# Decoder layer in f32 on one core: the first batch element's cross-attention output projection as seven block products, and its transposed weights copied by two engines

## The chip, the cores and the metric

The kernel runs on one core of one Trainium2 chip. The metric is the device time of one execution in microseconds (us). TensorE (PE in the profile, its weight loads PEld) does the matrix products, VectorE (DVE), ScalarE (ACT) and GpSimd (POOL) the elementwise work, and SyncE (SP) issues nearly all DMAs.

## The reference, cut to what matters

A decoder layer for a batch of 2, 512 tokens, width 512, all in f32: self-attention of 16 heads with block-scaled weights, then cross-attention on a context of 1024 rows in which each token keeps its 54 highest scores, then a gated feed-forward part. After each comes a residual sum and a layer norm. The piece that matters here is the end of the cross-attention:

```python
scores = coef * jnp.einsum('bsd,bnd->bsn', Q, K_mem)
thr = jax.lax.top_k(scores, clip_k)[0][..., -1:]
att = jax.nn.softmax(jnp.where(scores < thr, -jnp.inf, scores), axis=-1)
out = jnp.einsum('bsn,bnd->bsd', att, V_mem)      # 512 x 1024 by 1024 x 512
return out @ W_o.T                                # 512 x 512 by 512 x 512
x = _layernorm(x + that)
```

## The kernel before, in words

Most matrix products are done as **seven block products**: both operands are cut into 2 by 2 blocks, seven products of sums and differences of blocks take the place of the eight plain ones, and the results are put together by additions. `combine_a` and `combine_b` (lines 104 to 120) make the four sums of the left or of the right operand; `sums_a` (line 137) does it in steps, and overwrites one block. `seven` (line 170) issues the products for one block of 128 output rows by two column halves of 256:

- products 1, 6 and 7 build up in one PSUM bank `r`. After each of them ScalarE copies the bank's running state out into `u` (`keep`, line 197), and the next of the three has to wait for that copy.
- products 2 and 4, then 5 and 3, go to three quarters of a double bank `z`. When 2, 4 and 5 are there, `on_second` adds `z` and `u` on VectorE. Product 3 builds up on product 5 in the same place, so it waits until `on_second` has read it. It is left open (`rest`, line 222), and the next `seven`, or `close()`, issues it. Then `on_first` adds.
- with `late=True`, products 2 and 4 are issued ahead of product 1.

The program's order is not the order on the engines. A planner orders each engine's instructions when the kernel is built: in the trace POOL runs the sums of line 1214 at 689.7 us and those of line 1211 at 702.4 us, and matrix products of different calls alternate on PE. The order of the program acts as a priority.

The cross-attention of the **second** element (b = 1, at 863 to 903 us) uses seven block products throughout, the output projection too: `xattend` line 607 on. `xw["woc"]` (line 1222) are the sums of the output weights, made on GpSimd in place `v1`. The **first** element (b = 0, at 652 to 711 us) goes like this:

- `transpose_weights` (line 541): the 512 by 1024 softmax weights are transposed on PE, 32 transposes of 128 by 128 into PSUM (line 552); each group of four fills a bank, and ScalarE copies the bank to SBUF (line 555). There are 8 such copies. `combine_at` then makes the sums of the transposed weights on VectorE (lines 152 to 155).
- `xattend(0)` (line 578) is a generator. Its first step, `xav0_0`, is run at line 1036. Then come `project(last)`, the end of the self-attention of element 1; its layer norm; `turn_x(1)` (line 1039), which transposes element 1's activations with VectorE transposes and 16 small DMAs into `x1T`; `combine_turned` (line 1040, the sums `x1c`) and loads.
- at line 1043 the second half of `xattend(0)` follows: `xav0_1`, and then the output projection, which for b = 0 is **plain**: 4 token tiles by 4 chunks, 16 products of 128 by 128 by 512 (line 633) into banks `r` and `t`, in an order that uses the chunks `ot` 0, 2 and 3 before the last one, `ot` 1. VectorE adds each tile to the residual (line 642).
- then `layernorm(0)`, the transposition `x2T` and the sums `x2c` for element 0's feed-forward part, and on PE meanwhile `seven_xquery(1)` (products named xq, from `x1T`, `x1c` and the GpSimd sums `wqc`) and `seven_xscores(1)` (named xs).

Places in SBUF are shared by name: `wv` holds the sums `oc` of `project(last)` until its last product, `k0`, `q0`, `q1` hold keys and queries of attention heads, and later `ut` and `gt` of the feed-forward part.

Of the kernel before, what the change touches and what calls it, by code (L numbers as in the profile page):

```python
# [16 lines left out]
P = 128  # L17
# [7 lines left out]
def decoder_layer(  # L25
# [21 lines left out]
    nc = tc.nc  # L47
# [4 lines left out]
    NT = S // P  # L52
    NK = M // P
# [6 lines left out]
    HK, HS, HD = KD // 2, S // 2, D // 2  # L60
# [11 lines left out]
    def bank(tag, name):  # L72
        return ps.tile([P, 512], F32, tag=tag, name=name)
# [4 lines left out]
    def place(tag, shape, name):  # L78
        return sb.tile([P, *shape], F32, tag=tag, name=name)
# [21 lines left out]
    ALEFT = lambda a, c: {1: a[0], 2: a[1], 3: c[3], 4: a[3], 5: c[0], 6: c[1], 7: c[2]}  # L101
# [11 lines left out]
    def combine_b(eng, b, c):  # L113
        b00, b01, b10, b11 = b
        c = [c[:, n] for n in range(4)]
        eng.tensor_tensor(c[0], b01, b00, ALU.subtract)  # L116
        eng.tensor_tensor(c[1], b11, c[0], ALU.subtract)
        eng.tensor_tensor(c[2], b11, b01, ALU.subtract)
        eng.tensor_tensor(c[3], b10, c[1], ALU.subtract)
        return BRIGHT(b, c)  # L120

    def blocks(w):

        k, n = w.shape[1] // 2, w.shape[2] // 2
        return w[:, :k, :n], w[:, :k, n:], w[:, k:, :n], w[:, k:, n:]
# [11 lines left out]
    def sums_a(eng, a, c, steps):  # L137


        for n, w in enumerate(steps):  # L140
            a00, a01, a10, a11 = (f[:, w] for f in a)
            eng.tensor_tensor(c[0][n], a10, a11, ALU.add)
            eng.tensor_tensor(c[1][n], c[0][n], a00, ALU.subtract)
            yield
            eng.tensor_tensor(a10, a00, a10, ALU.subtract)
            eng.tensor_tensor(c[2][n], a01, c[1][n], ALU.subtract)
            yield
# [17 lines left out]
    def close():  # L165

        if open_product:
            open_product.pop()()

    def seven(name, stat, mov, cols, on_second, on_first, bias=(0.0, 0.0), late=False, piece=None, scale=1.0):  # L170


        n = seven_count[0] % 2
        seven_count[0] += 1
        r = bank("r", f"r{name}")[:, :HS]
        if piece:

            zs = [bank("t", f"z{name}_{i}")[:, :HS] for i in range(2)] + [double(f"z{name}", (4, HS))[:, 2, :]]
        else:
            z = double(f"z{name}", (4, HS))  # L180
            zs = [z[:, i, :] for i in range(3)]
        u = place(f"u{n}", (3, HS), f"u{name}")

        def product(i, o, start=True):
            left, right = chunks(stat[i]), chunks(mov[i])
            for k in range(len(left)):
                nc.tensor.matmul(  # L187
                    o,
                    left[k][:, cols],
                    right[k],  # L190
                    start=start and k == 0,
                    stop=k == len(left) - 1,
                    skip_group_check=not start,
                )

        def keep(i, at, scale=1.0):
            nc.scalar.activation(u[:, i, :], r, AF.Identity, bias=at, scale=scale)  # L197

        if late:
            product(2, zs[1])  # L200
            product(4, zs[0])
        product(1, r)
        keep(0, bias[0])
        if not late:
            product(2, zs[1])
        product(5, zs[2])
        product(6, r, False)
        keep(1, bias[0])
        close()
        product(7, r, False)  # L210
        keep(2, bias[1], scale)
        if piece:
            piece(zs[2], u[:, 2, :], 1, 1)
            piece(zs[1], u[:, 0, :], 0, 0)
        if not late:
            product(4, zs[0])
        if piece:
            piece(zs[0], u[:, 2, :], 1, 0)
        else:
            on_second(z[:, 0::2, :], u[:, 2:3, :].to_broadcast([P, 2, HS]))  # L220

        def rest():
            product(3, zs[2], False)
            if piece:
                piece(zs[2], u[:, 1, :], 0, 1)
            else:
                on_first(z[:, 1:3, :], u[:, 0:2, :])

        open_product.append(rest)

    res, rb, xts, xcs = {}, {}, {}, {}
# [118 lines left out]
    mems, memTs, xw, qts, sts, ats = {}, {}, {}, {}, {}, {}  # L350
# [10 lines left out]
    def load_mem(b):  # L361
        mems[b] = []
        for n in range(2):
            mt = place(f"{('mt', 'pt')[b]}{n}", (NK // 2, D), f"mem{b}_{n}")
            nc.sync.dma_start(
                out=mt,
                in_=mem[b, n * half_m : (n + 1) * half_m, :].rearrange("(k p) f -> p k f", p=P),
            )
            mems[b].append(mt)
# [171 lines left out]
    def transpose_weights(b, tags):  # L541

        at = []
        for k in range(NK):
            if k % (NK // 2) == 0:
                ath = place(tags[k // (NK // 2)], (NK // 2, S), f"at{b}_{k}")
                at.append(ath)
            if k % 2 == 0:
                trs = double(f"atr{b}_{k}")
            tr = trs[:, k % 2, :]  # L550
            for t in range(NT):
                nc.tensor.transpose(
                    tr[:, t * P : (t + 1) * P], sts[b, t][:, k * P : (k + 1) * P], ident
                )
            nc.scalar.copy(ath[:, k % (NK // 2), :], tr)
        ats[b] = [a[:, :, h] for a in at for h in (slice(0, HS), slice(HS, S))]

    def combine_mem(b, tags):
# [15 lines left out]
    def combine_at(b, tags):  # L574
        c = [place(tag, (NK // 2, HS), f"atc{b}_{n}") for n, tag in enumerate(tags)]
        ats[b] = sums_b(nc.vector, ats[b], c)

    def xattend(b, ot_tags):

        oth = [place(tag, (2, S), f"xo{b}_{n}") for n, tag in enumerate(ot_tags)]  # L580
        ot = [t[:, n, :] for t in oth for n in range(2)]
        o4, sums = [t[:, :, h] for h in (slice(0, HS), slice(HS, S)) for t in oth], []
        if b == 1:
            c12 = [place(f"p{n}", (HK, HS), f"xoc{n}") for n in range(2)]
            c4 = place("wqk0", (HK, HS), "xoc_4")

        def first(z, u, m):
            put(ot[m], z, u, b == 1)
            if b == 1:
                c = [f[:, m : m + 1] for f in (*c12, c4)]  # L590
                sums.append(sums_a(nc.vector, o4, [[f] for f in c], [slice(m, m + 1)]))
                next(sums[-1])
                for left in sums if m else ():
                    next(left)

        for m in range(HK):
            seven(
                f"xav{b}_{m}",
                mems[b],
                ats[b],  # L600
                slice(m * P, (m + 1) * P),
                lambda z, u, m=m: put(ot[HK + m], z, u, b == 1),
                lambda z, u, m=m: first(z, u, m),
            )
            yield
        close()
        if b == 1:
            stat = ALEFT(o4, (*c12, o4[2], c4))
            for s in range(NT // 2):

                def add(z, u, t):
                    o = res[b, t].rearrange("p (c f) -> p c f", c=2)
                    nc.vector.tensor_add(o, o, u)
                    nc.vector.tensor_add(o, z, o)

                seven(
                    f"xpo{b}_{s}",
                    stat,
                    xw["woc"],
                    slice(s * P, (s + 1) * P),  # L620
                    lambda z, u, s=s: add(z, u, 2 + s),
                    lambda z, u, s=s: add(z, u, s),
                    late=s == 0,
                )
            close()
            return

        order = [(t, k) for t in range(NT) for k in (0, 2, 3, 1)]
        if b == 0:
            order = [(0, 0), (0, 2), (0, 3), (1, 0), (1, 2), (1, 3), (0, 1), (1, 1)] + order[8:]  # L630
        po = [bank("rt"[t % 2], f"xpo{b}_{t}") for t in range(NT)]
        for t, k in order:
            nc.tensor.matmul(
                po[t],
                ot[k][:, t * P : (t + 1) * P],
                xw["wo"][:, k, :],
                start=(k == 0),
                stop=(k == 1),
                skip_group_check=True,
            )  # L640
            if k == 1:
                nc.vector.tensor_add(res[b, t], po[t], res[b, t])

# [394 lines left out]
    combine_turned(nc.vector, 1, "v0", "x1")  # L1040
    load_xw("wq", xwq, "cmb1", 1)
    load_mem(1)
    for _ in attended:
        pass
    combine_memT(1, ("wqk3", "wqk4", "ot1"))
# [173 lines left out]
    load_wdn(0, 1)  # L1219
    search1 = chain(search1, turn_weights(1, 2, ("ot0", "ot1"), ("cmb0", "cmb1"), ("v0", "work")))  # L1220
    def attended_early():
        xw["woc"] = combine_b(nc.gpsimd, blocks(xw["wo"]), place("v1", (4, HK, HD), "woc"))
        yield from xattend(1, ("ot0", "ot1"))

    hc = up(0, 1, nc.vector, search1, combine_wdn(0, 1), attended_early())
# [86 lines left out]
```

## Time and profile before

| what | value |
|---|---|
| median of 3 runs | 1084.7 us (1083.64 to 1084.9) |
| profiled execution: its own time | 1084.43 us |
| its span, first to last instruction | 1082.6 us (1.83 us lie around it) |
| mean granted clock of TensorE | 0.999 |
| DVE, ACT, POOL busy | 57%, 38%, 53% of the span |
| stretch of the transposes on PE | 652.04 to 659.36 us |
| from the first to the last product of line 633 | 692.95 to 710.13 us |

A line of a timeline holds the start, the duration, the engine, the line, the operation, the tiles (output, arrow, inputs) and how many instructions were merged; brackets hold the idle time just before and what ended it. Every f32 matrix product shows as two records on PE, so the 16 products of line 633 are 32 records and the 32 transposes happen to be 32. The duration of a PE record overlaps the next one; the distance from start to start is its price.

### The profile page before, as it was taken

How to read it: one execution, taken by the hardware profiler on the slowest of the kernel's cores; microseconds unless marked ns; L12 is line 12 of the kernel's file. 1: busy time of each engine (PE TensorE's matmuls, PEld its weight loads, DVE VectorE, ACT ScalarE, POOL GpSimd, SP SyncE). 2: the span in 40 equal slices, each digit the busy share in tenths (PEclk: the TensorE clock that was granted, in tenths of full speed). 3: DMA queues.
4: the chain of work that ended last, by engine and by line, in shares of the span. 5: the costliest groups of instructions: out<-in, count | busy, mean ns of one | idle time of the engine just before them, and what ended most of it. 6: DMA issues, size and time to landing. Idle time of an engine off the chain costs nothing.

```text
span 1082.6 us, 12783 instructions
## 1 busy us (share of the span) xinstructions
PE 1070.4 (99%) x4252; PEld 796.8 (74%) x4252; DVE 613.4 (57%) x1015; ACT 409.0 (38%) x882; POOL 575.2 (53%) x578
## 2 busy tenths in 40 slices
PE   9999999999999999999999999999999999999997
PEld 5676776677677677665666567778888888888886
DVE  6444345335434445643899774468999736554354
ACT  3444435335344533733444453222443214221121
POOL 4966626846845856514952654525565812264530
PEclk9999999999999999999999999999999999999999
DMA  9545455655554455536332447231214401422201
GB/s 350 156 127 173 157 155 181 192 158 152 191 177 115 155 178 151 192 80 180 137 117 78 117 133 257 82 113 39 96 65 132 136 21 49 165 80 79 95 20 39
DMA packets 66097, 142.71 MB, mean 132 GB/s; under 512 B 12528, under 2 KB 12528, under 8 KB 66032
## 3 DMA queue, kind: packets, MB, share of 16 engines
q1 hardware_dynamic: 65312, 139.80, 41.6%
q10 hardware_dynamic: 720, 2.10, 0.5%
q8 instruction: 34, 0.56, 0.2%
q14 instruction: 31, 0.25, 0.1%
HBM read 99.90 MB, written 2.10 MB: 94 GB/s over the span
## 4 chain that ended last, share of the span: by engine, by line
PE 84%; DVE 10%; ACT 2%; DMA 1%; POOL 1%; issue 1%; SPq 0%; ACTq 0%; DVEq 0%; POOLq 0%
PE sc L785 10%; PE av L830 9%; PE zqk L187 9%; PE zgu L187 7%; PE rqk L187 7%; PE rgu L187 5%; PE zo L187 5%; PE zv L187 5%; PE zpd L187 4%; PE ro L187 4%; PE rpd L187 3%; PE rv L187 3%; DVE work L493 3%; PE zxav L187 3%; DVE top L496 2%; PE xs L474 2%
## 5 line engine op out<-in xcount | busy, mean ns | idle before, releaser
L830 PE MATMUL av<-pt,v 128*128 128x512 f32 x256 | 121.9, 592 | 0.0
L796 DVE TENSOR_REDUCE nm<-sc 128x2 f32<-128x1024 f32 x63 | 77.0, 1223 | 76.0 <-PE sc L785 75.8
L785 PE MATMUL sc<-k,q 128*128 128x512 f32 x256 | 116.9, 598 | 0.0
L799 ACT ACTIVATE p<-sc,nm 128x512 f32<-128x512 f32 x128 | 86.9, 681 | 76.7 <-DVE nm L796 76.6
L810 DVE STREAM_TRANSPOSE tq<-p 128x512 f32<-128x512 f32 x128 | 84.9, 700 | 37.9 <-ACT p L807 33.0
L785 PEld LDWEIGHTS sc<-k,q 128*128 128x128 f32 x256 | 47.3, 190 | 62.6 <-issue 51.3
L807 ACT ACTIVATE p<-p,sm 128x512 f32<-128x512 f32 x128 | 85.4, 715 | 1.6 <-DVE sm L806 1.4
L107 POOL TENSOR_TENSOR wc<-wgu 128x256 f32<-128x256 f32 x32 | 25.0, 781 | 112.8 <-PE zgu L187 69.1
L684 POOL TENSOR_TENSOR wqk<-wqk,sqk 128x512 f32<-128x512 f32 x52 | 66.1, 1290 | 33.6 <-DMA wqk<-in_wqk 20.7
L197 ACT ACTIVATE ugu<-rgu 128x256 f32<-128x256 f32 x96 | 36.2, 379 | 102.7 <-PE rgu L187 100.4
L830 PEld LDWEIGHTS av<-pt,v 128*128 128x128 f32 x256 | 48.6, 190 | 29.7 <-issue 25.8
L187 PE MATMUL rgu<-x2c,wc 128*128 128x256 f32 x256 | 66.1, 380 | 1.0 <-ACT ugu L197 1.0
L187 PE MATMUL rqk<-x0c,wc 128*128 128x256 f32 x248 | 65.0, 384 | 0.3 <-ACT uqk L197 0.2
L496 DVE MAX8 top<-work 128x8 f32<-128x1024 f32 x48 | 58.6, 1221 | 0.9
L848 ACT ACTIVATE ot<-av,bqkv_sb 128x512 f32<-128x512 f32 x28 | 19.2, 687 | 101.9 <-PE av L830 101.9
L187 PEld LDWEIGHTS rgu<-x2c,wc 128*128 128x128 f32 x256 | 48.3, 190 | 8.7 <-ACT ugu L197 1.5
L187 PEld LDWEIGHTS rqk<-x0c,wc 128*128 128x128 f32 x248 | 45.1, 189 | 12.2 <-ACT uqk L197 5.1
L107 POOL TENSOR_TENSOR wc<-wqk 128x256 f32<-128x256 f32 x31 | 22.7, 733 | 59.0 <-PE zqk L187 58.2
L116 POOL TENSOR_TENSOR otc<-ot 128x512 f32<-128x512 f32 x7 | 8.9, 1272 | 81.4 <-PE zv L187 81.4
L1136 DVE TENSOR_TENSOR gt<-zgu,ugu 128x512 f32<-128x512 f32 x32 | 21.9, 684 | 47.6 <-PE zgu L187 47.6
L493 DVE MATCH_REPLACE8 work<-top,work 128x1024 f32<-128x1024 f32 x40 | 48.3, 1209 | 0.0
L748 DVE TENSOR_TENSOR q<-zqk,uqk 128x512 f32<-128x512 f32 x31 | 21.3, 688 | 41.5 <-PE zqk L187 41.5
(313 smaller groups left out, 2477.9 us busy)
## 6 DMA issues: line engine op xcount, KB each, us to landing
pt<-tq SPq DMA_DIRECT2D x512, 64.0 KB, 2.0
wgu<-in_wgu SPq DMA_DIRECT2D x32, 512.0 KB, 3.3
wqk<-in_wqk SPq DMA_DIRECT2D x26, 512.0 KB, 5.9
sqk<-in_wqk_s SPq DMA_DIRECT2D x26, 512.0 KB, 4.2
wdn<-in_wdn SPq DMA_DIRECT2D x8, 1024.0 KB, 5.8
sv<-in_wv_s SPq DMA_DIRECT2D x14, 512.0 KB, 6.2
wv<-in_wv SPq DMA_DIRECT2D x7, 1024.0 KB, 5.2
wo<-in_wo SPq DMA_DIRECT2D x7, 1024.0 KB, 5.8
```

The source lines that it names most:

```text
L107: eng.tensor_tensor(c[0], a10, a11, ALU.add)
L187: nc.tensor.matmul(o, left[k][:, cols], right[k], start=start and k == 0, stop=k == len(left) - 1, skip_group_check=not start,)
L197: nc.scalar.activation(u[:, i, :], r, AF.Identity, bias=at, scale=scale)
L493: nc.vector.match_replace(work, top, src, LOWEST)
L496: nc.vector.max(top, work)
L684: eng.tensor_tensor(part[:, w], codes[:, w], sct[:, w], ALU.mult)
L785: nc.tensor.matmul(pair[n], q[:, (t + n) * P : (t + n + 1) * P], k, start=True, stop=True,)
L796: nc.vector.reduce_max(nms, scs, axis=AX.X, negate=True)
L799: nc.scalar.activation(pr, pair[t % 2], AF.Exp, bias=nms[:, t % 2 : t % 2 + 1], accum_out=sm,)
L807: nc.scalar.activation(pr, pr, AF.Copy, scale=sm)
L810: nc.vector.transpose(tq[:, :, :, t, :].rearrange("p n k c -> p k n c"), pr.rearrange("p (k n a) -> p k n a", n=NB, a=BLK),)
L830: nc.tensor.matmul(av, vs[u // GH][:, k, j * P : (j + 1) * P], pt[:, :, k, :], start=(k == 0), stop=(k == NT - 1),)
```

## The change

For b = 0 the output projection takes the path that b = 1 had. The attention output's sums go to places `q0`, `q1`, `k0`; the sums of the output weights are made once more for b = 0, in place `wv`, on GpSimd, ahead of the second half of `xattend(0)`. The plain projection is gone. Of the 8 copies of the transposed weights, ScalarE does those with even k, VectorE those with odd k.

```diff
-            nc.scalar.copy(ath[:, k % (NK // 2), :], tr)
+            copy = nc.vector.tensor_copy if k % 2 else nc.scalar.copy
+            copy(ath[:, k % (NK // 2), :], tr)
...
+    def combine_wo(b, tag):
+        xw["woc"] = combine_b(nc.gpsimd, blocks(xw["wo"]), place(tag, (4, HK, HD), f"woc{b}"))
...
-        if b == 1:
-            c12 = [place(f"p{n}", (HK, HS), f"xoc{n}") for n in range(2)]
-            c4 = place("wqk0", (HK, HS), "xoc_4")
+        c12 = [place(f"{'qp'[b]}{n}", (HK, HS), f"xoc{b}_{n}") for n in range(2)]
+        c4 = place(("k0", "wqk0")[b], (HK, HS), f"xoc{b}_4")
...
             put(ot[m], z, u, b == 1)
-            if b == 1:
-                c = [f[:, m : m + 1] for f in (*c12, c4)]
-                sums.append(sums_a(nc.vector, o4, [[f] for f in c], [slice(m, m + 1)]))
-                next(sums[-1])
-                for left in sums if m else ():
-                    next(left)
+            c = [f[:, m : m + 1] for f in (*c12, c4)]
+            sums.append(sums_a(nc.vector, o4, [[f] for f in c], [slice(m, m + 1)]))
+            next(sums[-1])
+            for left in sums if m else ():
+                next(left)
...
-        order = [(t, k) for t in range(NT) for k in (0, 2, 3, 1)]
-        if b == 0:
-            order = [(0, 0), (0, 2), (0, 3), (1, 0), (1, 2), (1, 3), (0, 1), (1, 1)] + order[8:]
-        po = [bank("rt"[t % 2], f"xpo{b}_{t}") for t in range(NT)]
-        for t, k in order:
-            nc.tensor.matmul(
...
-            if k == 1:
-                nc.vector.tensor_add(res[b, t], po[t], res[b, t])
...
     load_mem(1)
+    combine_wo(0, "wv")
     for _ in attended:
         pass
...
-        xw["woc"] = combine_b(nc.gpsimd, blocks(xw["wo"]), place("v1", (4, HK, HD), "woc"))
+        combine_wo(1, "v1")
```

The loop `for s in range(NT // 2)` with `seven(f"xpo{b}_{s}", ...)` of lines 608 to 625 stays as it was, and now runs for both elements.

More of the change, by code (lines that the diff above doesn't have):

```diff
@@ L606, in xattend, with add @@
         close()
[L607 to L626, printed above, removed]
-        order = [(t, k) for t in range(NT) for k in (0, 2, 3, 1)]
-        if b == 0:
-            order = [(0, 0), (0, 2), (0, 3), (1, 0), (1, 2), (1, 3), (0, 1), (1, 1)] + order[8:]
-        po = [bank("rt"[t % 2], f"xpo{b}_{t}") for t in range(NT)]
-        for t, k in order:
[L633 to L639, printed above, removed]
-            )
-            if k == 1:
-                nc.vector.tensor_add(res[b, t], po[t], res[b, t])
+        stat = ALEFT(o4, (*c12, o4[2], c4))
+        for s in range(NT // 2):
+            def add(z, u, t):
+                o = res[b, t].rearrange("p (c f) -> p c f", c=2)
+                nc.vector.tensor_add(o, o, u)
+                nc.vector.tensor_add(o, z, o)
+            seven(
+                f"xpo{b}_{s}",
+                stat,
+                xw["woc"],
+                slice(s * P, (s + 1) * P),
+                lambda z, u, s=s: add(z, u, 2 + s),
+                lambda z, u, s=s: add(z, u, s),
+                late=s == 0,
+            )
+        close()
     phases = [(0, 0), (0, 1)] + [(g, b) for b in range(B) for g in range(1, NG)]
```

## The prediction

> **What bounds the kernel now.** I read the busy times first, then PE's own waits.
>
> ```profile
> PE 1070.4 (99%) x4252; PEld 796.8 (74%) x4252; DVE 613.4 (57%) x1015; ACT 409.0 (38%) x882; POOL 575.2 (53%) x578
> ```
> ```profile
> PE idle L86 <- DVE eps L90: 1.2, 1, 1.2
> PE rgu L187 <- ACT ugu L197: 1.0, 2, 0.7
> ...
> PE atr L552 <- ACT at L555: 0.4, 1, 0.4
> ```
>
> PE is busy 99% of the span, and each of its waits for another engine sums to 1.2 us or less. So a microsecond of products taken off PE is a microsecond of time if PE finds its next operands ready, and a bubble if it doesn't. The change touches two places; I read PE's timeline at the first and the chain that ended last at the second.
>
> ```profile
> 652.04 1.04 PE L552 MATMUL atr<-ident,s 128*128 128x128 f32 x8
> 653.46 0.66 PE L552 MATMUL atr<-ident,s 128*128 128x128 f32 x4 [0.38 <-ACT at L555]
> ...
> 659.36 3.60 PE L830 MATMUL av<-pt,v 128*128 128x512 f32 x8
> ```
> ```profile
> 693.11 0.86 PE xpo L633 x2
> ...
> 695.69 1.72 PE xpo L633 x4
> 697.41 1.73 PE zxav L187 x8
> 699.14 11.16 PE xpo L633 x26
> 710.29 0.86 PE rxq L187 x4
> ```
>
> In the first, PE waits for ScalarE to empty a bank. In the second PE runs without a hole, and six records of the projection sit between products of xav0_1, where they cover waits.
>
> **Part 1, the copies.** From 652.04 to 659.36 us, 7.32 us, PE does 32 transposes and 14 records of 256 columns. Transposes cost 0.108 each (four from 658.06 to 658.49), records of 256 columns 0.2157 (eight in the chain's 1.73): 3.45 + 3.02 = 6.47. So **0.85 us** is lost to the copies. ScalarE's eight take 0.586 each, behind an `ot_last` eviction of 0.69. Afterwards each engine has four. VectorE idles there (5.35 and 2.37 us before its sums `atc`), so they are hidden. No row shows a VectorE copy out of PSUM; the nearest, the 512-wide add that reads PSUM (L393, 0.69), and ScalarE's 0.586 bound it. The next thing, `av`, needs DMAs whose last issue ends at 654.5, plus 2.0 to landing: 656.5, before PE gets there at 658.5. Between nothing and -0.85 I take **-0.7**, since the bank pair is still filled and emptied alternately.
>
> **Part 2, the products.** Removed are 32 records of 512 columns at 11.16/26 = 0.4292: 13.73 us. Added are 2 x 7 x 2 = 28 products, 56 records at 0.2157: 12.08. **-1.65 us** of PE work.
>
> **Part 3, waits inside the new chain.** The plain order needed nothing back from ScalarE or VectorE; the seven need it at three places.
> (a) Between products 7 and 3 of xav0_1 PE waits for a copy and an add, from 695.53 to about 696.9, 1.37 us. Six plain records covered it and the step before. Now product 2 and product 1 of both halves can give only their first chunk there (the second needs `ot` 3 or `ot` 1): 3 x 0.43 = 1.29 in all. Bounds 0 to 0.6, taken 0.3.
> (b) After xav0_1's last product (698.97) `ot` 1 is put by 699.86; product 2's second chunk and product 4 cover 1.29. Taken 0.
> (c) The last product 3 waits for the add `on_second`. The second element shows it:
>
> ```profile
> 899.06 1.03 PE L187 MATMUL zxpo<-woc,xo 128*128 128x256 f32 x4
> 899.92 1.03 PE L187 MATMUL rgu<-x2T,wgu 128*128 128x256 f32 x4
> 900.78 0.59 PE L187 MATMUL zgu<-x2T,wgu 128*128 128x256 f32 x2
> 901.30 1.13 PE L187 MATMUL zxpo<-wo,xoc 128*128 128x256 f32 x4
> ```
>
> From 899.92 to 901.30, 1.38 us, the feed-forward part fills in. For the first element the only filler is xq, and that needs `x1T`:
>
> ```profile
> 693.60 13.06 SPq L289 DMA_DIRECT2D x1T<-x1Tt  x16
> ```
>
> The last issue ends at 706.66, plus a median 2.0 to landing: 708.7, or 708.0 shifted by part 1. PE would be at the hole at 710.13 - 1.65 - 0.7 - 0.86 = 706.9. So xq comes too late to cover it: bounds 0 (`x1T` lands earlier) to 1.4, taken **1.0**, since xq can fill the hole's end. (a) and (c): **+1.3**.
>
> **Part 4, the other engines.** VectorE adds 8 sums of 0.42 (L142 to L146), and 8 adds of 0.69 take the place of 4: +6.1 us. From 699.2 to 726.4 it is busy 17.9 of 27.2, so the other 9.3 hide this; without cover see rival 2. ScalarE: 6 keeps of 0.38 for four copies of 0.586, both beside PE, and it idles 15.1 us before xq. POOL: four sums of 1.26, 5.04. They need `wv`, free when project(last) ends at 685.9. POOL is idle there:
>
> ```profile
> 672.84 1.27 POOL L155 TENSOR_TENSOR mT<-memT,mT 128x512 f32<-128x512 f32 x1
> 689.74 2.52 POOL L142 TENSOR_TENSOR mc<-mem,mem 128x512 f32<-128x512 f32 x2 [15.63 <-PE zxav L187]
> ```
>
> So they run from 685.9 to 690.9, before the projection at 693, and push `mc` (needed after 863) and `wqc` (702.4 to 707.5, needed by PE near 710) back by 1.2: nothing. No DMA is added. Downstream everything hangs on PE, and VectorE's long search starts when PE's xs products arrive, so it moves along: 0, bounds -0.5 to +1.
>
> **Sum:** -0.7 - 1.65 + 1.3 = -1.05 on the profiled execution's 1084.43 = 1083.4. That execution lies 0.27 under the median of 1084.7, which gives 1083.65. I say **1083.5**.
>
> **Rivals.**
> 1. **No holes.** `x1T` lands in time (its 16 issues took 13.06 us here, those of `x2T` 10.01), or the planner finds other filler. Then -0.85 - 1.65 = -2.5: **1082.0**. For it: PE's waits everywhere else are near zero in chains of the same kind. Against: at this one place the filler arrives at 708.
> 2. **VectorE becomes the bound** from 699 to 726 (the slower side). Its two-input SBUF sums stretch when POOL works at the same time:
>
> ```profile
> 664.64 1.75 DVE L118 TENSOR_TENSOR otc<-ot_last 128x512 f32<-128x512 f32 x1
> ```
> ```profile
> 733.41 0.69 DVE L118 TENSOR_TENSOR x2c<-x2T 128x512 f32<-128x512 f32 x1
> ```
>
> The first ran beside POOL's `mT` sums (1.71 instead of 1.26), the second with POOL idle; 256-wide ones go from 0.42 to 0.83 (L1106). POOL is busy 14.35 of 17.2 us in 693 to 710.2, and would be more so. Six new sums stretched by 0.41 and four L613 by 1.06 are 6.7 us. VectorE then has 17.9 + 5.3 + 6.7 = 29.9 us for 25.0 us of PE's new pace, 4.9 too much: -2.35 + 4.9 = +2.55, **1087.2**. It decides when more than half of these ten stretch. Against: PSUM-reading adds next to POOL kept 0.69 (L642 at 702.6).
>    The Trainium skill, "GPSIMD Engine Reference", section 1, says that GpSimd shares its SBUF interfaces with VectorE and contends with VectorE instructions that have two SBUF inputs. That speaks against moving work to both engines at once. By the rows with POOL idle the sum is -1.05; by the rule at full strength it is rival 2's +2.55. The trace shows both kinds of rows, also two-input ones that kept 0.68 while POOL stretched instead (648.37).
> 3. **The weight sums come late.** If the planner puts the `mc` sums first, POOL is taken until 698.9 and `woc` ends at 703.9, while product 4 wants it at 698.8: +5.1, in all about +4: **1088.5**. Against: `wv` frees 3.8 us before `mc`'s place.
> 4. **The copies do nothing**, PE's stretch being held by something else: +0.7 on my sum, 1084.2. This lies inside my forecast's own range.
>
> **How the numbers follow.** Forecast with some holes (4 included) 0.48, its own range 1082.5 to 1085.2 (holes of 0 to 2, copies 0 to -0.85, +1 downstream); rival 1 0.27; rival 2 0.18; rival 3 0.07. The range for 8 in 10 takes in rival 1 and rival 2's price: 1081.6 to 1087.4. A measurement of this kernel can tell about 0.2%, 2.2 us, from no change. Faster by over that (below 1082.5): most of rival 1 and a little of the forecast, 0.27. Slower (above 1086.9): most of rival 2, rival 3, 0.22. Within: 0.51.
>
> **What would show it.** Right: 56 records named xpo at 0.216; the transposes' stretch near 6.5; PE idle about 1 us just before the last xpo product or the first xq; `woc` on POOL before 691. Wrong: xpo without a hole (rival 1), L613 or L142 to L146 over 0.8 us and PE waiting for qt or x1c (rival 2), PE waiting for woc (rival 3). If PE loses time after 746, a step I priced at zero failed.

## The result, and the profile after

| | median | runs | against before |
|---|---|---|---|
| before | 1084.54 us (1083.06 to 1086.74) | 18 | |
| after | 1086.22 us (1085.32 to 1087.91) | 18 | ratio 1.0016, 95% interval 1.001 to 1.0022 |

The change costs 1.7 us, where a gain of about 1 us was forecast. The profiled execution took 1086.21 us with a span of 1084.4 us, against 1084.43 and 1082.6.

The busy times don't show where: PE is as busy as before to the tenth of a us. A record's duration runs on past the point at which the next one could start, so small holes don't appear in it.

```profile
PE 1070.4 (99%) x4276; PEld 801.1 (74%) x4276; DVE 625.6 (58%) x1031; ACT 409.0 (38%) x884; POOL 581.3 (54%) x582
```

PE's waits for other engines say more. The columns are the total in us, how often, and the longest:

```profile
PE zxpo L187 <- DVE res L615: 1.3, 2, 0.8
...
PE rxpo L187 <- ACT uxav L197: 0.5, 1, 0.5
PE atr L552 <- ACT at L556: 0.4, 1, 0.4
```

The first two did not exist before. The third is the wait that the alternating copies were to take away, and it is unchanged. In PE's timeline of after, the waits lie in the new projection:

```profile
695.97 0.70 PE L187 MATMUL rxpo<-wo,xo 128*128 128x256 f32 x2 [0.47 <-ACT uxav L197]
...
700.26 1.33 PE L187 MATMUL zxpo<-woc,xoc 128*128 128x256 f32 x4
701.42 1.03 PE L187 MATMUL rxpo<-woc,xoc 128*128 128x256 f32 x4
...
705.31 1.03 PE L187 MATMUL rxpo<-woc,xoc 128*128 128x256 f32 x4
707.09 1.13 PE L187 MATMUL zxpo<-wo,xoc 128*128 128x256 f32 x4 [0.75 <-DVE res L615]
...
710.64 0.59 PE L187 MATMUL zxq<-x1T,wq 128*128 128x256 f32 x2
711.78 1.13 PE L187 MATMUL zxpo<-wo,xoc 128*128 128x256 f32 x4 [0.54 <-DVE res L615]
```

A hole is the distance from one start to the next, less 0.2157 us for each record. From 705.31 to 707.09 are 1.78 us for four records of 0.86: a hole of 0.92. In the same way 0.71 ahead of 711.78, 0.30 ahead of 701.42, and 0.63 and 0.30 around 695.97. Waiting for `res L615` means that a product 3 wants its place in PSUM, and VectorE's `on_second` has not read it yet. VectorE's timeline shows why it is late:

```profile
676.04 0.43 DVE L142 TENSOR_TENSOR xoc<-xo,xo 128x256 f32<-128x256 f32 x1
...
699.46 1.37 DVE L142 TENSOR_TENSOR xoc<-xo,xo 128x256 f32<-128x256 f32 x1
700.86 0.83 DVE L143 TENSOR_TENSOR xoc<-xoc,xo 128x256 f32<-128x256 f32 x1
...
702.48 0.94 DVE L146 TENSOR_TENSOR xoc<-xo,xoc 128x256 f32<-128x256 f32 x1
703.35 2.89 DVE L614 TENSOR_TENSOR res<-res,uxpo 128x512 f32<-128x512 f32 x2
706.34 0.69 DVE L615 TENSOR_TENSOR res<-zxpo,res 128x512 f32<-128x512 f32 x1
```

The same line 142 on the same shape takes 0.43 at 676 and 1.37 at 699. Between them GpSimd went from idle to busy, as its timeline shows:

```profile
672.33 1.28 POOL L155 TENSOR_TENSOR mT<-memT,mT 128x512 f32<-128x512 f32 x1
685.65 1.27 POOL L116 TENSOR_TENSOR woc<-wo 128x512 f32<-128x512 f32 x1 [12.05 <-PE zo L187]
...
699.28 1.27 POOL L146 TENSOR_TENSOR mc_p<-mem,mc 128x512 f32<-128x512 f32 x1
...
703.98 1.71 POOL L107 TENSOR_TENSOR wqc<-wq 128x512 f32<-128x512 f32 x1
```

GpSimd pays too: 1.71 instead of 1.27. The four sums (1.37, 0.83, and 0.94 twice) and the four adds of `u` (1.21 and 1.61, merged above to 2.89, then 0.96 and 1.34) take 9.20 us instead of 4 x 0.42 + 4 x 0.69 = 4.44. The adds that read PSUM (L615, L393) stay at 0.69 throughout.

Where the time went, in starts on PE: the three landmarks are the last group of `av` ahead of the transposes, the first product xpo and the first product rgu of element 0's feed-forward part.

| kernel | av to xpo | xpo to rgu | rgu to the end |
|---|---|---|---|
| before | 43.48 | 52.87 | 336.8 |
| after | 43.66 | 54.90 | 336.8 |

So the copies cost 0.18 and the projection with what follows it 2.03, and nothing changes behind 746 us. After's profiled execution reached `av` 0.38 us earlier, which makes 1.83, and the two executions differ by 1.78. With 1.65 us less work on PE, its holes grew by 2.03 + 1.65 = 3.7 us: 1.03 around 696 (product 3 of xav0_1, with 0.10 that follows it), 0.30 at 701, 1.02 and 0.82 at the two products 3 of xpo (each with 0.10 behind it), and 0.55 more than before in xq and xs.

### The profile page after: what moved, and what is told of

Same layout as the page of the kernel before. It is cut to its first block, busy times and chain, and to the rows that moved or that the text cites. A ratio compares the mean times of both kernels' runs of the same rounds, so it can differ in the third digit from the quotient of the medians.

```text
span 1084.4 us, 12862 instructions
## 1 busy us (share of the span) xinstructions
PE 1070.4 (99%) x4276; PEld 801.1 (74%) x4276; DVE 625.6 (58%) x1031; ACT 409.0 (38%) x884; POOL 581.3 (54%) x582
## 4 chain that ended last, share of the span: by engine, by line
PE 82%; DVE 13%; ACT 2%; POOL 1%; issue 1%; DMA 1%; SPq 0%; ACTq 0%; DVEq 0%; POOLq 0%
PE sc L769 10%; PE av L814 9%; PE zqk L187 9%; PE zgu L187 7%; PE rqk L187 7%; PE zo L187 5%; PE rgu L187 5%; PE zv L187 5%; PE zpd L187 4%; PE ro L187 4%; DVE work L493 3%; DVE top L496 3%; PE rv L187 3%; PE rpd L187 3%; PE zxav L187 3%; PE xs L474 2%
```

## The experiments

My theory after the result: the loss is VectorE's stretched sums in the projection, that is, GpSimd's weight and context sums running beside them; the copies are worth nothing because something other than ScalarE's speed holds the transposes. Rivals: the loss is the order of the waits in the seven products themselves, whatever GpSimd does, or the two parts hurt each other. From the third experiment on, the expectations call the rival of the order of the two adds theory 2 and the stretched sums theory 3; for the transposes, theory 1 is that a pair of banks is handed over as one. Each ratio is against runs of the kernel before on the same chip.

**The two parts alone.** The copies alone, the projection as before:

```diff
-            nc.scalar.copy(ath[:, k % (NK // 2), :], tr)
+            copy = nc.vector.tensor_copy if k % 2 else nc.scalar.copy
+            copy(ath[:, k % (NK // 2), :], tr)
```

> The kernel before with the copies of the transposed weights shared by ScalarE and VectorE, projection plain as before. Theory 1 (the two banks of a pair are handed over as one, so the transposes still wait for each copy in turn, and VectorE's copy of 0.69 us is slower than ScalarE's 0.59): PE's stretch from the first transpose to av stays at 7.3 to 7.5 us, time equal to before within 0.3 us. Rival (the copies were worth 0.7 us as predicted, and the projection hid it): stretch 6.5 to 6.8, time 0.6 to 0.9 us under before.

Measured: 1084.48 us, ratio 1.0 (0.9991 to 1.0009). The projection alone, all copies on ScalarE:

```diff
-            copy = nc.vector.tensor_copy if k % 2 else nc.scalar.copy
-            copy(ath[:, k % (NK // 2), :], tr)
+            nc.scalar.copy(ath[:, k % (NK // 2), :], tr)
```

> The kernel after with all copies back on ScalarE. Theory 1 (the loss is all in the projection's waits): time as the kernel after, 1.4 to 2.0 us over before. Rival (the VectorE copies cost something themselves): 0.3 us or more under the kernel after.

Measured: 1085.9 us, ratio 1.0012 (1.0004 to 1.0021). From av to xpo the first takes 43.65 and the second 43.47 us, and from xpo to rgu the second takes 54.95: each part shows in its own stretch what the whole change shows there. The projection is the loss, and the copies give nothing.

**The order of the two adds.** Product 3 waits for the add that reads `z`. Here that add comes ahead of the add of `u`, for both elements:

```diff
-                nc.vector.tensor_add(o, o, u)
                 nc.vector.tensor_add(o, z, o)
+                nc.vector.tensor_add(o, o, u)
```

> The kernel after, but each residual update of the projection adds z (PSUM) first and u (SBUF) second, in both elements, so that product 3 waits for one add that needs no copy. Theory 2 (order of the two adds makes the holes ahead of the two products 3, 0.9 and 0.7 us): both holes close, 1.2 to 1.8 us under the kernel after, about equal to before. Theory 3 (VectorE is the bound because its two-input SBUF adds stretch beside GpSimd): the adds of u still take 1 to 1.45 us, VectorE comes late all the same, and at most 0.6 us is won.

Measured: 1084.99 us, ratio 1.0003 (0.9994 to 1.0012). Two waits closed and a new one opened, as PE's timeline of this kernel shows:

```profile
706.06 1.03 PE L187 MATMUL rxpo<-woc,xoc 128*128 128x256 f32 x4
706.93 1.03 PE L187 MATMUL zxpo<-wo,xoc 128*128 128x256 f32 x4
...
720.16 1.03 PE L187 MATMUL zxq<-x1c,wq 128*128 128x256 f32 x4
722.19 1.13 PE L187 MATMUL rxq<-x1c,wqc 128*128 128x256 f32 x4 [1.00 <-ACT uxq L197]
```

The first product 3 now follows at once (0.87 after four records of 0.86). But later xq waits 1.00 us for a copy on ScalarE, which the planner has put behind element 0's layer norm (four instructions, 2.93 us, on ScalarE). So the 1.2 us gained in the median is less than the 1.6 us of the two holes that closed. This is what theory 2 had forecast, both holes closed and 1.2 to 1.8 us under the kernel after, although the four sums stretched as before (1.39, 0.83, 0.94, 0.94); theory 3's "at most 0.6 us" did not come. The two holes thus need both conditions: sums and adds that stretch, and an order in which the add that frees product 3's place comes last. In the trace the gain is smaller than in the median: from xpo to rgu this kernel takes 54.41 us, 0.49 less than after.

**GpSimd kept out of the way.** Nothing in the seven products changes; the weight sums `wqc` go to another place and so run before the projection, and the sums of element 1's context wait until later (the small copy of `behind()` into their place is what holds them back):

```diff
-    seven_xquery(1, "xT1", "xc1", ("sc1", "p0"))
+    seven_xquery(1, "cmb0", "xc1", ("sc1", "p0"))
...
-    def combine_mem(b, tags):
+    def combine_mem(b, tags, behind=None):
...
+        if behind:
+            nc.gpsimd.tensor_copy(c1[:, ::2, 0:1], behind())
...
-    for _ in chain(combine_wdn(0, 0, lambda: xcs[0][4][:, :, 0, 0:1]), combine_mem(1, ("wqk2", "sc2", "p2", "p3"))):
+    for _ in combine_wdn(0, 0, lambda: xcs[0][4][:, :, 0, 0:1]):
...
+    late_mem = combine_mem(1, ("wqk2", "sc2", "p2", "p3"), lambda: xcs[0][4][:, :, 0, 0:1])
...
-    hc = up(0, 0, nc.gpsimd, search1)
+    hc = up(0, 0, nc.gpsimd, search1, late_mem)
+    for _ in late_mem:
+        pass
```

> The kernel after, with GpSimd kept quiet during the projection: the query weight sums go to another place in SBUF, so that they run before 692 us, and the sums of the second element's context are held back until x2c is there. Theory 3 (stretch beside GpSimd): sums back to 0.42 us, adds of u to 0.69, the holes ahead of the products 3 shrink by 1 us or more, time 1.0 to 1.8 us under the kernel after, unless the sums held back cost something later. Theory 2 (order of the adds): sums and adds shorten, but product 3 still waits for copy, add of u and add of z: at most 0.6 us under the kernel after.

Measured: 1091.25 us, ratio 1.0064 (1.0051 to 1.0076), a miss of mine: the two product 3 waits are gone, but PE then waits elsewhere. PE's waits of this kernel:

```profile
PE zgu L187 <- POOL wc L107: 4.4, 1, 4.4
```

The context sums ran on GpSimd from 747.9 to 757.7 us, ahead of the feed-forward weight sums `wc` that PE was about to need. So the next version holds them behind the first `ut` of the feed-forward part and spreads them over its steps, for the changed kernel and for the kernel before:

```diff
+    def late_mem():
+        for _ in combine_mem(1, ("wqk2", "sc2", "p2", "p3"), lambda: uts[0][:, :, 0:1]):
+            yield
+            yield
+
+    late_mem = late_mem()
...
```

> The kernel before, with GpSimd kept quiet during the plain projection (query weight sums early, the second element's context sums spread later). Theory 3 (stretch beside GpSimd hurts only the new sums and adds): the plain projection has no two-input SBUF work on VectorE on its path, so time equal to before within 0.5 us. Rival (a quiet GpSimd helps everything): 0.8 us or more under before.

> The kernel after, with GpSimd kept quiet as in the first such run, but the context sums spread over four steps of the feed-forward part so that they hold nothing up. Theory 3: the stretch from the first transpose to the first feed-forward product stays some 1.8 us shorter than in the kernel after, and with no loss later the time is 1.2 to 1.9 us under the kernel after, about that of before. Theory 2 (order of the two adds): at most 0.6 us under the kernel after.

Measured: 1083.36 us, ratio 0.9992 (0.9983 to 1.0001) with the plain projection; 1084.11 us, ratio 0.9997 (0.9988 to 1.0006) with the change. The changed kernel thus goes from 1.7 us over before to 0.3 under, which is not to be told from before. The plain kernel's median fell too, by 1.0 us (0.1 over to 1.8 under): that is the rival's "0.8 us or more", not the "within 0.5" that I expected. Its trace shows no gain in the projection (xpo to rgu 53.32 us, 52.87 in before), and its 1.0 us stays unexplained; the last kernels below test it again. In the changed kernel GpSimd is idle from 697.9 to 713.9 us and the sums are short again. VectorE's timeline of it:

```profile
700.07 0.42 DVE L142 TENSOR_TENSOR xoc<-xo,xo 128x256 f32<-128x256 f32 x1
...
703.21 0.69 DVE L616 TENSOR_TENSOR res<-res,uxpo 128x512 f32<-128x512 f32 x1 [1.59 <-ACT uxpo L197]
```

and PE's, at the same two products 3 as above:

```profile
705.62 1.03 PE L187 MATMUL rxpo<-woc,xoc 128*128 128x256 f32 x4
706.48 1.13 PE L187 MATMUL zxpo<-wo,xoc 128*128 128x256 f32 x4
...
710.04 0.59 PE L187 MATMUL zxq<-x1T,wq 128*128 128x256 f32 x2
710.56 1.13 PE L187 MATMUL zxpo<-wo,xoc 128*128 128x256 f32 x4
```

0.92, 0.71 and 0.30 have become 0.00, 0.09 and 0.00. From xpo to rgu it takes 53.07 instead of 54.90: 1.83 us. The kernel that came out at 1091.25 us has the same 53.07 in this stretch. The rest of the holes is as in the change, the 0.9 us around 696 among it.

The z-first order on top of the quiet GpSimd:

> As e8_quiet_after, and z added first, u second. Theory 3 alone explains the holes: equal to e8_quiet_after within 0.4 us. Theories 2 and 3 each explain a part (the wait for copy and two adds remains when VectorE is quick): 0.3 to 0.9 us under e8_quiet_after, which would be 0.3 to 1.0 us under before.

Measured: 1084.03 us, ratio 0.9998 (0.999 to 1.0007), the same as without it, as theory 3 had it. With the sums short, there is nothing left to close at product 3, and the wait for `uxq` (1.06 us here) comes with the order: in the trace xpo to rgu takes 54.04 us, 0.97 more than without it, which the medians don't show.

**The transposes.** Two neighbouring groups of transposes share a `double` tile of two banks, and the profile names the copy as what the next group waits for. The kernel after, with ScalarE copying the even groups and VectorE the odd ones, shows which groups these are. The rows are of PE, ScalarE and VectorE:

```profile
653.08 0.65 PE L552 MATMUL atr<-ident,s 128*128 128x128 f32 x4 [0.38 <-ACT at L556]
652.45 1.06 ACT L556 COPY at<-atr 128x512 f32<-128x512 f32 x2
653.84 0.69 DVE L556 COPY at<-atr 128x512 f32<-128x512 f32 x1 [3.86 <-PE atr L552]
```

ScalarE's two copies, of even groups, run on end from 652.45, so the eight transposes that PE did from 651.67 on were the first halves of two pairs, groups 0 and 2. The second half of a pair is begun only at 653.08, when ScalarE's first copy (0.59 of the 1.06) is done, and VectorE's first copy starts at 653.84, when both of ScalarE's are over. So at the start the two engines copy in turn and not side by side. In the next two kernels each group has a bank of its own, with alternating copies and, as control, with all copies on ScalarE; the projection is plain in both. The edit changes a second thing with it: the groups leave the tiles named `z`, which the seven products use too, for `r` and `t`.

```diff
-            if k % 2 == 0:
-                trs = double(f"atr{b}_{k}")
-            tr = trs[:, k % 2, :]
+            tr = bank("rt"[k % 2], f"atr{b}_{k}")
```

> The kernel before, copies shared by ScalarE and VectorE, and each group of four transposes in a bank of its own (four banks in turn) in place of pairs. Theory 1 (the pair, handed over as one, kept the copies from running side by side): PE's stretch from the first transpose to av falls from 7.3 to 6.5 to 6.8 us, the shared copies now count. Rival (it is the copies' own length or VectorE's slowness): stretch stays at 7.2 or more.

> The kernel before, each group of four transposes in a single bank of its own instead of half of a pair, all eight copies still on ScalarE. If the pair is what serialises the stage: the transposes run with small holes (ScalarE's eight copies of 0.586 us are 4.7 us for 3.45 us of transposes), and the time is 0.7 to 1.4 us under the kernel before, near the 1082.98 that two copying engines gave. If the second engine is what brought that: equal to before within 0.3 us.

Measured: 1082.98 us, ratio 0.9987 (0.9978 to 0.9996), with both engines; 1083.91 us, ratio 0.9994 (0.9985 to 1.0003), with ScalarE alone. PE's timeline of the first:

```profile
641.97 0.49 PE L550 MATMUL atr<-ident,s 128*128 128x128 f32 x3
...
652.29 3.38 PE L550 MATMUL atr<-ident,s 128*128 128x128 f32 x29
...
658.97 3.60 PE L829 MATMUL av<-pt,v 128*128 128x512 f32 x8
```

29 transposes run without a hole (the next product starts at 655.51, so 0.111 each), and three have moved into an earlier hole. From av to xpo: 43.48 before, 43.65 with alternating copies in the pair, 42.66 with own banks and ScalarE alone, 42.41 with own banks and both engines. So the banks are worth 0.82 us in this stretch, of which 0.33 are the three transposes that left it for the earlier hole, and the second engine 0.25 more; within the pair it is worth nothing. How much of the 0.82 comes from ending the pair and how much from leaving `z` was not tried apart. In ScalarE's timeline of the control one sees the eight copies run on end, at 0.5 us each, while the transposes ahead of them need 0.43 for a group:

```profile
652.94 4.00 ACT L553 COPY at<-atr 128x512 f32<-128x512 f32 x8
```

The control is 0.5 us under before, between the two ranges expected of it (0.7 to 1.4 under, or within 0.3). The medians of these two kernels differ by 0.9 us, but their intervals overlap, and the traces account for 0.25 to 0.5 of it.

**All together.** The change with own banks; then with own banks and the quiet GpSimd; and the plain projection with own banks, the quiet GpSimd and copies by both engines. The edits are those above.

> The change as it is, with only the transposes given banks of their own. If the stretched sums of the projection are the whole loss and the copies are then worth what was forecast or more: +1.7 for the change less 0.17 less 1.4, so +0.1 to +0.4 against the kernel before. If an earlier PE only meets a larger hole at the projection: +1 or more.

> The whole change, the second element's weight and context sums kept off GpSimd's way during the output projection, and the transposes in banks of their own. If the two remedies add: 1084.11 - 1084.37 = -0.26 for the quiet GpSimd, -1.4 for banks and copies, less the +0.17 of the copies in the pair: -1.6 to -1.9 against the kernel before. If they touch the same hole (PE reaches the projection earlier and waits there instead): -0.3 to -0.8.

> The plain projection of the kernel before, with the same quiet GpSimd, banks of their own and copies by both engines. If the seven block products are worth nothing even with GpSimd quiet (their 1.65 us eaten by 1.5 us of holes): the time is that of the same kernel with the seven products, and 1.4 to 2.4 us under before. If the seven products are worth something there, this one is 0.5 to 1.5 us slower than its companion with them.

Measured, in this order: 1084.8 us, ratio 1.0003 (0.9995 to 1.0012); 1082.77 us, 0.9984 (0.9975 to 0.9993); 1082.95 us, 0.9986 (0.9977 to 0.9994). The two remedies add up: +0.4 and -1.6 us, as the first branch of each expectation had it. These kernels also test whether a quiet GpSimd helps everything. With own banks it is worth 2.0 us to the changed projection (+0.4 to -1.6), as it was worth 1.9 to the kernel after, but only 0.1 to the plain one with both engines copying (-1.4 to -1.5). The medians of the last two do not differ: they show no gain from the seven products even where GpSimd is out of their way. In the traces the kernel with them takes 53.07 us from xpo to rgu, its plain companion 53.86. What is left of its holes is as in the other quiet kernel: 0.64 and 0.29 around 695 us, and 0.82 in xq and xs between 719 and 723 us. The best three kernels (own banks with both engines; the same with the quiet GpSimd, with and without the seven products) are faster than before and than after, and not to be told from each other.

One caution on the stretch xpo to rgu. In the six kernels with the plain projection that were profiled here it takes 52.87, 53.77, 53.32, 53.55, 53.32 and 53.86 us, with holes of 0.2 to 0.6 in xq that come and go. VectorE's rows in these six show why. The last sum of `x1c` (line 119) takes 0.67, 1.10, 0.67, 0.90, 0.67 and 1.21 us, by how it meets GpSimd's next weight sums `wc`, whose start differs from kernel to kernel, and PE's hole ahead of the product that needs it is 0.06, 0.49, 0.06, 0.28, 0.05 and 0.61. Likewise a tiny instruction of the layer norm with two SBUF inputs (line 340) takes 0.17 in before and 0.62 in the other five, and only those five have a further hole of 0.36 or 0.37 in xq. Both fit the same conflict. In the three with the changed projection beside a busy GpSimd and the adds in their old order it takes 54.90, 54.95 and 54.92. The profiled execution of before, which met neither, was the lowest of its kind. (From rgu to the end all the kernels with the same work there lie between 335.9 and 337.0, the quiet ones among them.) Against the mean of the six, 53.45, the projection costs 1.5 us, and with 0.18 for the copies that is the 1.7 of the medians.

## Why the prediction was wrong

Of the 2.7 us between the forecast's -1.05 and the measured +1.7, the copies make 0.9 and the projection 1.8, by the stretches of the traces.

**Part 1, the copies, taken as -0.7: +0.18.** The 0.85 us lost was read rightly, and so was each engine's load: the VectorE copy took 0.69 (the row chosen for it was 0.69) and ScalarE's 0.586. What failed is "-0.7, since the bank pair is still filled and emptied alternately": with the pair kept, nothing is gained, while own banks gain 0.82 without a second engine. The wait named in the profile, PE for ScalarE's copy of a group, was a wait for a shared tile, not for a slow engine: the second group of a pair was begun only when the first had been copied (653.08 us above), so the two engines did not work side by side on a pair. This is what rival 4 said, and with +0.7 on the sum it would have been a forecast of 1084.2.

**Part 2, the products, -1.65:** right. The products have the price of 0.2157 a record; the 56 records lie in the timeline.

**Part 3, the waits in the chain, taken as +1.3: +3.7 against the profiled execution of before, 3.1 against the mean of the six plain kernels.** With GpSimd quiet the same difference is 1.3 (53.07 - 53.45 + 1.65), the very figure of the forecast, but by luck: the places were others. (a) was taken as 0.3 with a bound of 0.6, and 0.93 was measured, in the quiet kernels too. Of the three fillers of 0.43 that I counted, two were placed ahead of product 7, where nothing waits, and the third, at 695.97, had itself to wait for the copy `uxav`. (b) was taken as 0 and cost 0.30, because product 5 waited for the first sum of line 142, 1.37 instead of 0.42. (c) was taken as 1.0 for a wait that xq could not fill. It was 0.71 at that place, and xq filled part of it: `x1T` had landed in time. A second one of 0.92, at the first product 3, was not in my list. I compared with the second element, whose sums run without GpSimd beside them.

**Part 4, "the other 9.3 hide this": this is the step that failed.** I set 6.1 us of added VectorE work against 9.3 us of idle time between 699.2 and 726.4. The added work stretched by 4.8 us beside GpSimd, and, more to the point, the idle time was not where the work was: from 699.46 to 707.0 us VectorE has no gap, and in that time two products on PE wait for it. The forecast weighed the stretching as rival 2 at 0.18, and its price of 1087.2 was not far from the 1086.2 measured. The stretching is what cost the time: undoing GpSimd's presence alone took 1.83 of the 2.03 us of this stretch away. But the way to the price was another, and its nearness is in part luck. Rival 2 made VectorE the bound of the whole stretch, 4.9 us too slow; from 699.2 to 728.2 us it was busy 25.7 of 29.0, with 3.3 us to spare, and the loss came from three waits of PE, 0.30 behind a stretched sum and 0.92 and 0.71 behind the two adds. Its sign was to be PE waiting for `qt` or `x1c`; the profile names `res` instead. Its stretching was put too high, 6.7 us against 4.8, and its condition, "more than half of these ten", was met: the four sums of the first half, at 676 to 679 us, ran while GpSimd was idle, the four of the second half and the four adds stretched.

I named "PSUM-reading adds next to POOL kept 0.69" as evidence against. That is true (L615 kept 0.69 too), but the sums do not read PSUM.

The Trainium skill, "GPSIMD Engine Reference", section 1, was weighed against this change and proved right: GpSimd's SBUF interfaces are shared with VectorE, and instructions of VectorE with two SBUF inputs contend. The rows here agree on who is hit (two SBUF inputs: 0.43 to 1.37 and 0.69 to 1.61; a PSUM input: none). The Trainium skill, "SBUF — State Buffer", section "SBUF: two separate sides", calls it an exclusive lock, held for a whole instruction. The rows fit that, but for a part of each record. From 699.28 us on, by start and duration, GpSimd's instructions end at 700.55, 701.41, 702.27, 703.14 and 704.01 and VectorE's four sums at 700.83, 701.69, 702.56 and 703.42. The two alternate: each sum of VectorE ends 0.28 to 0.29 us after one of GpSimd, each of GpSimd 0.58 to 0.59 after one of VectorE. Undisturbed they take 0.42 and 0.72. So all but about 0.14 us of each record excludes the other engine, an estimate from these rows.

**Rivals 1 and 3.** Not rival 1: the holes did not close, although `x1T` came in time. Not rival 3: `woc` ran from 685.65 to 690.7 us as forecast, and PE waited for no weight sum.

What stays open: why the median of the plain kernel fell by 1.0 us with a quiet GpSimd in one pair of kernels and by 0.1 in the other, and whether a different order around product 3 of xav0_1 would close its 0.93 us, which was not tried.

## What to carry to other kernels

Idle time of an engine hides added work only if it lies between the work's inputs and the product that waits for it: lay the added instructions out in time, one by one, against that product. Price them by rows in which the other engines do what they will do there; in these traces a row with GpSimd idle was a lower bound for VectorE's two-input sums. And where PE waits for a copy out of PSUM, ask first what tile is handed over, since a second copying engine gave nothing until each group had its own bank, and 0.25 us then.

## What the hardware did that I had not expected

The same VectorE sum of two SBUF operands, 128 by 256 in f32, took 0.43 us with GpSimd idle and 0.83 to 1.37 beside it; of 128 by 512, 0.69 and 0.96 to 1.61. GpSimd's own went from 1.27 to 1.71, and its 128 by 256 from 0.72 to as much as 1.23. In the kernel before, from 693 to 707 us, VectorE had no instruction of two SBUF inputs beside the same GpSimd work: adds with a PSUM input and norm statistics stayed at 0.67 to 0.69, with GpSimd at 1.27 to 1.28. The change did not add a busy engine, but the first instructions there that disturb each other.
